# Moving convolutions between the stages of a pipelined Haar-mixing network: four channels come a batch earlier, empty ticks take put-off convolutions, and the last mixing has its first products ahead of its second ones

## The chip, the cores and the metric

The kernel runs on one core of a Trainium2 chip. Its engines work side by side[...]: PE (TensorE, the matmuls), DVE (VectorE), ACT (ScalarE), POOL (GpSimd, not used here) and SP (SyncE, which only issues transfers here; ACT issues some too). The metric is the device time of one execution in microseconds (us). The kernel before takes 2989.25 us, the median of three runs (2988.33 to 2990.84).

## The reference

The input x has 4 batches of 64 channels of 256 x 256 fp32 values. Four layers follow one another. Layers 0, 1 and 3 are long convolutions of each channel with a kernel that is an outer product of two filters, so that each is two triangular Toeplitz products, along one axis and then along the other:

```python
hx = _implicit_filter(z, Xw1, ..., t, deltas)      # 256 positions x 64 channels, from a small sine network
hy = _implicit_filter(z, Yw1, ..., t, deltas)
k = jnp.einsum('ijk,imk->ijmk', hx, hy)[0]         # one 256 x 256 kernel per channel
k_f = jnp.fft.rfft2(k, s=(512, 512)) / 512
u_f = jnp.fft.rfft2(x, s=(512, 512))
y = jnp.fft.irfft2(u_f * k_f, s=(512, 512))[..., :256, :256]
out = y + x * bias[:, None, None]
```

Layer 2 works on the 2-D Haar transform and mixes the 64 channels of a batch, so it needs all channels of the batch:

```python
f1 = haar2d(x)
for i in range(2):
    f4 = jnp.einsum('bchw,oc->bohw', f1 * v[i], conv_w[i])
    acc = acc + jnp.sign(f4) * jax.nn.relu(jnp.abs(f4) - tau[i])
y = haar2d(acc, inverse=True) + x
```

## The kernel before, in words

**Stages.** Each batch goes through three stages. `convolutions` does layers 0 and 1 for each channel and the forward Haar transform, and writes the Haar coefficients to DRAM (`coef`) and what the skip connection needs to `keep`. `mixing` does the channel mixing of layer 2 in 64 groups of four rows of coefficients, and adds the results up in the large tile `z`, which lies in SBUF. `inverse` takes one channel after the other out of `z`, does the inverse Haar transform, adds the skip connection and does layer 3 (`last`), or puts layer 3 off: it then stores the channel to `late`, and `convolution` does layer 3 later, under the mixing of another batch. `put_off` says which channels: every third from channel 2 on, 21 in each of batches 0 to 2, 63 in all.

**One convolution layer** is two contractions (`contract`, L186): `first` multiplies by one Toeplitz matrix on PE into a bank `pa` of PSUM, and ACT copies it to `a` (L198); `second` multiplies `a` by the other matrix into `py`, and DVE adds the bias term (L211). A contraction is four matmuls in source, two of 256 and two of 128 columns (L189, L190); [...] a contraction is eight instructions in the profile. The Toeplitz tile (`t`) is loaded by SP from the padded filter in DRAM. A channel of `convolutions` has four contractions, a put-off convolution two. The channel of `convolutions` also has a step of Haar sums on DVE (`pairs`, L256 and L257; the other levels by groups of four channels, `levels`, L266 and L267), a split of the result into two parts (`split`, L277 on ACT, L278 on DVE), and the transform along the partitions on PE (`down`, L285, copied by ACT at L293, stored by SP at L294).

**One group of mixing** is `mix` (four matmuls, L334, into `px`, which has two buffers; then a scaling of `px` into `f4`, of which DVE does the first part, L351, and ACT `n_act` of 16 slices, L353), `shrink` (Abs and Sign on ACT, L359 and L360; subtraction on DVE, L361), `signed` (DVE, L366) and `add` (DVE, into `z`, L370). `n_act` is 12 for batches 0 to 2 and 6 for batch 3. `mag` and `f4` have two buffers.

**One channel of inverse** is `fetch` (load of `r` from `keep`, and ACT takes the channel out of `z` as `zc`, L387), `rows` (PE, `pw`, L394 and L395; ACT and DVE split it, L397 and L398), `cols` (PE, `pu`, L407; DVE adds the skip, L411, and interleaves, L414 and L415), then `last` or the store to `late`. Before channel 0, `butterfly` (L219 to L221) combines the two halves of `z`.

**The order** is written out by hand in ticks: `at(tick, place, run, unit)` collects every step, and at the end of the kernel the steps are sorted by tick, then by place, and run in that order; the recording layer below still moves instructions of an engine past one another where their inputs allow. `mixing(b, start, ...)` puts group g at tick `start + g`. `spread(begin, end, n)` spreads n units evenly over ticks. The convolutions of batch b + 1 are spread over the ticks of the mixing of batch b, so that PE, DVE and ACT have both kinds of work; the 63 put-off convolutions are spread over the last mixing, since there are no further batches. With the numbers of this kernel:

| batch | mixing, ticks from start to end | under it | ticks of these |
|---|---|---|---|
| 0 | 77 to 144 | 64 convolutions of batch 1 | 64 to 145, 82 ticks |
| 1 | 208 to 275 | 64 convolutions of batch 2 | 205 to 276, 72 ticks |
| 2 | 339 to 406 | 64 convolutions of batch 3 | 336 to 407, 72 ticks |
| 3 | 470 to 537 | 63 put-off convolutions | 468 to 538, 71 ticks |

So eight ticks of 72 have no new convolution in the mixing of batches 1 and 2. The inverse of batch b begins at the end of its mixing. `after` (inside `convolutions`) spreads the Haar steps of the last two groups of channels threefold where they come after `border`, the end of the mixing: they then lie between channels of the inverse. Buffers that the change concerns: `in` (three: loads of x and of `late`), `toep` (five), `co` (two: coefficients on the way to `coef`, and `y3` on the way to the output), `sp` (one), `y` (three).

Of the kernel before, what the change touches and what calls it, by code (L numbers as in the profile page):

```python
# [9 lines left out]
F32 = mybir.dt.float32  # L10
# [6 lines left out]
B, C, S, EMB, ORD = 4, 64, 256, 33, 64  # L17
P = 128
ROW = S + P

GT = 4
BUFS = {"res": 1, "y": 3, "co": 2}

INV_2PI = float(np.float32(1.0 / (2.0 * math.pi)))
# [13 lines left out]
def conv_seq_kernel(ctx, tc, x, fz, fw, bias, decay, haar, haar_row, factors, vt, taut, wmix, out):  # L38
# [14 lines left out]
    nc = tc.nc  # L53

    const = ctx.enter_context(tc.tile_pool(name="const", bufs=1))
# [8 lines left out]
    psx = ctx.enter_context(tc.tile_pool(name="psx", bufs=2, space=PSUM))  # L64


    hbt = const.tile([P, P], F32, name="hbt")
    hb = const.tile([P, P], F32R, name="hb")
    hbr = const.tile([P, P], F32R, name="hbr")
    hrow = const.tile([P, 2, P], F32, name="hrow")  # L70
# [7 lines left out]
    sd = zpool.tile([P, 8, 2, 2, P], F32, name="sd")  # L78
    keep = [dram.tile([C, P, 2, 2, P], F32, name=f"keep{b}") for b in range(B)]
    coef = [dram.tile([2, C, P, S], F32, name=f"coef{b}") for b in range(B)]  # L80
    scales = dram.tile([S // 4 // GT, P, 2, GT, 16], F32, name="scales")
    pads = [dram.tile([C, 2, ROW], F32, name=f"pad{layer}") for layer in range(3)]
# [7 lines left out]
    def part(n, parts=P):  # L90
        free[0] += n
        return room[:parts, free[0] - n : free[0]]
# [52 lines left out]
        return [load, *steps, end, warm]  # L145

    def constants():
        signs = part(P)
        nc.sync.dma_start(hbt, haar[0])
        nc.sync.dma_start(signs, haar[1])  # L150
        nc.sync.dma_start(hrow, haar_row)
        nc.vector.memset(wb, 0.0)
        for r in range(2):
            nc.sync.dma_start(wb[r * C : (r + 1) * C, r, :], wmix)
        nc.scalar.copy(hb, signs)
        nc.scalar.copy(hbr, hbt)

    def tables():
# [10 lines left out]
        def scale(i):  # L169
            nc.vector.tensor_mul(vts[:, i], vts[:, i], fac[:, i])  # L170
            nc.sync.dma_start(
                scales[:, :, i].rearrange("n p g j -> p n (g j)"), vts[:, i].rearrange("p (n g) j -> p n (g j)", g=GT)
            )
# [12 lines left out]
    def contract(ps, src, t):  # L186

        for m in range(2):
            nc.tensor.matmul(ps[:, m, :], src[:, 0, m * P : (m + 1) * P], t[:, ::-1], start=True, stop=False)  # L189
            nc.tensor.matmul(ps[:, m, P:], src[:, 1, m * P : (m + 1) * P], t[:, : P - 1 : -1], start=False, stop=True)  # L190
# [12 lines left out]
    def second(b, st, key, layer, res, new, tag, ahead=None):  # L203
        def run(c):
# [4 lines left out]
            contract(ps, s[key], s[layer][:, 1, :])  # L209
            y = io.tile([P, 2, S], F32, name=f"{new}_{b}_{c}", tag=tag, bufs=BUFS[tag])  # L210
            nc.vector.scalar_tensor_tensor(y, s[res], bsb[:, layer, c : c + 1], ps, ALU.mult, ALU.add)  # L211
# [15 lines left out]
    def at(tick, place, run, unit):  # L227
        events.append((tick, place, len(events), run, unit))
# [5 lines left out]
                if stage is not None:  # L234
                    at(tick + s, -s, stage, unit)

    def convolutions(b, ticks, in_parts=(), border=None):


        st = {}  # L240

        def after(tick, n):
            return tick if border is None or tick < border or n < C // 4 - 2 else border + 3 * (tick - border)

        def load(c):
            xt = io.tile([P, 2, S], F32, name=f"x_{b}_{c}", tag="in", bufs=3)
            nc.sync.dma_start(xt, x[b, c].rearrange("(k p) w -> p k w", p=P))
            st[c] = {"x": xt, 0: toeplitz(0, c, f"t0_{b}_{c}")}

        last_second = second(b, st, "a1", 1, "y0", "y1", "res")  # L250

        def pairs(c):
            last_second(c)
            v = st.pop(c)["y1"].rearrange("p k (w e) -> p k w e", e=2)
            t = sd[:, c % 8]
            nc.vector.tensor_add(t[:, :, 0, :], v[:, :, :, 0], v[:, :, :, 1])  # L256
            nc.vector.tensor_sub(t[:, :, 1, :], v[:, :, :, 0], v[:, :, :, 1])  # L257
            nc.scalar.dma_start(keep[b][c], t)

        def levels(steps):  # L260
            def run(n):
                t = sd[:, n % 2 * 4 : n % 2 * 4 + 4]
                for step in steps:
                    v = t[:, :, :, 0, :].rearrange("p c k (w e) -> p (c k) w e", e=2 * step)
                    even, odd = v[:, :, :, 0], v[:, :, :, step]
                    nc.vector.tensor_sub(odd, even, odd)  # L266
                    nc.vector.scalar_tensor_tensor(even, even, 2.0, odd, ALU.mult, ALU.subtract)  # L267

            return run

        parts = {}

        def split(c):

            w = parts[c] = mx.tile([P, 2, 2, S], F32R, name=f"sp_{b}_{c}", tag="sp", bufs=1)
            t = sd[:, c % 8].rearrange("p k e w -> p k (e w)")
            nc.scalar.copy(w[:, 0], t)  # L277
            nc.vector.tensor_tensor(w[:, 1], t, w[:, 0].bitcast(F32), ALU.subtract)  # L278

        def down(c):  # L280
            ps = bank(f"pz_{b}_{c}")
            flat = "p k w -> p (k w)"
            if c in in_parts:
                for i in range(2):
                    nc.tensor.matmul(  # L285
                        ps.rearrange(flat), hbr, parts[c][:, i].rearrange(flat), start=(i == 0), stop=(i == 1)
                    )
            else:
                nc.tensor.matmul(
                    ps.rearrange(flat), hbt, sd[:, c % 8].rearrange("p k e w -> p (k e w)"), start=True, stop=True  # L290
                )
            t = io.tile([P, 2, S], F32, name=f"co_{b}_{c}", tag="co", bufs=BUFS["co"])
            nc.scalar.copy(t, ps)  # L293
            nc.sync.dma_start(coef[b][:, c].rearrange("k p w -> p k w"), t)  # L294

        stream(
            [load, first(b, st, "x", 0, "a0"), second(b, st, "a0", 0, "x", "y0", "y", ahead=1), first(b, st, "y0", 1, "a1"), pairs],
            ticks,
        )
        for n in range(C // 4):  # L300
            end = ticks[4 * n + 3] + 4
            for s, steps in enumerate([(1,), (2, 4), (8, 16, 32, 64)]):
                at(after(end + 1 + s, n), 1, levels(steps), n)
            for j in range(4):
                if 4 * n + j in in_parts:
                    at(after(end + 3 + j, n), 2, split, 4 * n + j)
                at(after(end + 4 + j, n), 2, down, 4 * n + j)
        return after(ticks[-1] + 11, C // 4 - 1)

    def mixing(b, start, n_act):  # L310
# [3 lines left out]
        def load(g):  # L314
            f = mx.tile([P, 2, S], F32, name=f"f_{b}_{g}", tag="f", bufs=3)
            nc.sync.dma_start(f, coef[b].rearrange("k c p w -> (k c) p w")[:, 2 * g : 2 * g + 2])
            st[g] = {"f": f}
            if g % GT == 0:
                t = mx.tile([P, 2, GT, 16], F32, name=f"vt_{b}_{g}", tag="vt")
                nc.sync.dma_start(t, scales[g // GT])  # L320
                st["vt", g // GT] = t

# [54 lines left out]
    def inverse(b, start, put_off):  # L377
# [25 lines left out]
        def cols(c):  # L403
            ps = psm.tile([P, 2, 2, P], F32, name=f"pu_{b}_{c}", tag="mm")
            flat = "p m e w -> p (m e w)"
            for i in range(2):
                nc.tensor.matmul(  # L407
                    ps.rearrange(flat), hb, st[c]["w"][:, i].rearrange(flat), start=(i == 0), stop=(i == 1)
                )
            t = io.tile([P, 2, 2, P], F32, name=f"t_{b}_{c}", tag="res", bufs=BUFS["res"])  # L410
            nc.vector.scalar_tensor_tensor(t, st[c]["r"], 0.5, ps, ALU.mult, ALU.add)  # L411
            u = io.tile([P, 2, S], F32, name=f"u_{b}_{c}", tag="y", bufs=BUFS["y"])
            v = u.rearrange("p m (w e) -> p m w e", e=2)
# [16 lines left out]
    def last(b, st):  # L430
        return [
            first(b, st, "u", 2, "a3"),
            second(b, st, "a3", 2, "u", "y3", "co"),
            lambda c: nc.scalar.dma_start(out[b, c].rearrange("(k p) w -> p k w", p=P), st.pop(c)["y3"]),
        ]

    def convolution(which, ticks):

        for (b, c), tick in zip(which, ticks):
            st = {}  # L440

            def load(c, b=b, st=st):
                u = io.tile([P, 2, S], F32, name=f"v_{b}_{c}", tag="in", bufs=3)
                nc.sync.dma_start(u, late[b, c])
                st[c] = {"u": u, 2: toeplitz(2, c, f"t2_{b}_{c}")}

            for s, stage in enumerate([load, *last(b, st)]):
                at(tick + s, -s, stage, c)


    def spread(begin, end, n=C):
        return [begin + i * (end - begin - 1) // (n - 1) for i in range(n)]


    put_off = range(2, C, 3)

    one, two, three = filters(0, nc.scalar), filters(1, nc.scalar), filters(2, nc.sync)
    one[0]()
# [10 lines left out]
            at(tick, 3, lambda unit, do=do: do(), 0)  # L469

    groups = S // 4
    ready = convolutions(0, range(C), in_parts=range(C))
    ahead = C
    start = ready + 3
    for b in range(B):
        mixing(b, start, 12 if b + 1 < B else 6)
        end = start + groups + 3
        if b + 1 < B:
            ready = convolutions(b + 1, spread(ahead, end + 2), in_parts=range(C), border=end)
        else:  # L480
            convolution(
                [(i, c) for i in range(B - 1) for c in sorted(put_off)], spread(start - 2, end + 2, (B - 1) * len(put_off))
            )
        inverse(b, end, put_off if b + 1 < B else ())

        start = max(end + C, ready + 3)
        ahead = start - 3
    for _, _, _, stage, unit in sorted(events, key=lambda e: e[:3]):
        stage(unit)

# [108 lines left out]
```

## Time and profile before

| what | us |
|---|---|
| median of three runs | 2989.25 |
| profiled execution | 2989.2 |
| its span, first to last instruction | 2987.4 |
| PE busy | 2919.9 (98%) |
| DVE busy | 2551.9 (85%) |
| ACT busy | 2156.5 (72%) |
| first mix of batches 0, 1, 2, 3 starts at | 458.7, 1096.5, 1776.5, 2450.7 |
| last add of batches 0, 1, 2, 3 starts at | 877.9, 1554.5, 2234.3, 2733.7 |

The granted clock of TensorE was 1.00 over the span. Times inside the profile count from the first instruction. A row of the timeline has the start, the length, the engine, the line, the operation, output<-input with shapes, the number of instructions merged into the row, and in brackets the idle time ahead of it with what ended it. A row of the stage view has the stretch, the busy time of PE, PEld (weight loads), DVE, ACT and POOL with the number of instructions, TensorE's clock, the share of the DMA engines and GB/s. [...]

### The profile page before, as it was taken

The numbers are of one execution on the slowest core, as the hardware profiler recorded it, in microseconds if no ns is written. First come the engines' busy times: TensorE is split into PE (matmuls) and PEld (weight loads), VectorE is DVE, ScalarE is ACT, GpSimd is POOL, SyncE is SP. The second block draws the span as 40 slices with busy tenths as digits, with TensorE's granted clock in tenths as the row PEclk, the third lists the DMA queues.
The fourth block names the chain that finished last, engine by engine and source line by source line (L and its number), as shares of the span: only waits on it lengthen the run. The fifth ranks groups of instructions, "written<-read, shape, count | busy, mean of one in ns | idle before, by whom it ended". The sixth has DMA issues, their size and how long they took to land. (4 is left out here: it accounts for less than half of the span.)

```text
span 2987.4 us, 51999 instructions
## 1 busy us (share of the span) xinstructions
PE 2919.9 (98%) x16950; PEld 2610.5 (87%) x16950; DVE 2551.9 (85%) x4576; ACT 2156.5 (72%) x5005; POOL 0.2 (0%) x4
## 2 busy tenths in 40 slices
PE   7999999999999999999999999999999999999999
PEld 6899988888888888888888988888888988888998
DVE  4766778999998879999989879999998889998776
ACT  1333338999986758989886758989886768887554
POOL 0000000000000000000000000000000000000000
PEclk9999999999999999999999999999999999999999
DMA  4877777766667876676777776676677877777676
GB/s 146 245 234 229 230 231 210 210 200 199 210 201 243 249 219 203 207 209 203 208 213 236 253 224 196 209 211 204 206 211 235 255 238 231 231 232 220 212 210 187
DMA packets 562496, 649.72 MB, mean 217 GB/s; under 512 B 44369, under 2 KB 447412, under 8 KB 562100
## 3 DMA queue, kind: packets, MB, share of 16 engines
q1 hardware_dynamic: 446132, 494.94, 58.0%
q10 hardware_dynamic: 116096, 151.46, 14.2%
q8 instruction: 137, 2.24, 0.3%
q14 instruction: 131, 1.07, 0.1%
HBM read 426.77 MB, written 219.48 MB: 216 GB/s over the span
## 5 line engine op out<-in xcount | busy, mean ns | idle before, releaser
L189 PE MATMUL py<-t,a 128*128 128x256 f32 x3072 | 923.3, 382 | 17.8 <-ACT a L198 8.6
L198 ACT COPY a<-pa 128x512 f32<-128x512 f32 x768 | 473.3, 617 | 442.2 <-PE pa L190 298.2
L190 PEld LDWEIGHTS py<-t,a 128*128 128x128 f32 x3072 | 583.4, 190 | 79.3
L353 ACT ACTIVATE f<-px,vt 128x64 f32<-128x64 f32 x2688 | 589.7, 351 | 75.7 <-DVE f L351 75.3
L190 PE MATMUL py<-t,a 128*128 128x128 f32 x3072 | 590.0, 274 | 0.0
L189 PEld LDWEIGHTS py<-t,a 128*128 128x128 f32 x3072 | 491.6, 191 | 69.5 <-ACT a L198 32.0
L334 PE MATMUL px<-wb,f 128*128 128x256 f32 x2048 | 504.3, 382 | 19.6 <-ACT f L353 19.6
L334 PEld LDWEIGHTS px<-wb,f 128*128 128x128 f32 x2048 | 362.1, 190 | 67.2 <-ACT f L353 32.1
L361 DVE TENSOR_TENSOR mag<-mag,vt 128x1024 f32<-128x1024 f32 x256 | 312.7, 1222 | 18.8 <-ACT mag L359 16.6
L366 DVE SCALAR_TENSOR_TENSOR mag<-mag,f 128x1024 f32<-128x1024 f32 x256 | 312.8, 1222 | 4.4 <-DVE sd L266 0.3
L397 ACT CAST w<-pw 128x512 fp32r<-128x512 f32 x256 | 150.2, 587 | 226.5 <-PE pw L395 214.6
L189 PE MATMUL pa<-t,y 128*128 128x256 f32 x1024 | 306.6, 381 | 2.5 <-DVE y L211 1.6
L189 PE MATMUL pa<-t,x 128*128 128x256 f32 x1024 | 305.6, 380 | 1.5 <-issue 1.5
L359 ACT ACTIVATE mag<-f 128x1024 f32<-128x1024 f32 x256 | 282.9, 1105 | 21.1 <-DVE z L370 7.0
L387 ACT COPY zc<-z 128x512 f32<-128x512 f32 x256 | 282.4, 1104 | 2.3 <-ACT w L397 1.9
L360 ACT ACTIVATE f<-f 128x1024 f32<-128x1024 f32 x256 | 273.2, 1067 | 13.1 <-DVE sd L257 5.7
L278 DVE TENSOR_TENSOR sp<-sd,sp 128x512 fp32r<-128x512 f32 x256 | 176.6, 690 | 92.6 <-ACT sp L277 91.9
L211 DVE SCALAR_TENSOR_TENSOR y<-x,bsb,py 128x512 f32<-128x512 f32 x256 | 191.0, 746 | 55.5 <-PE py L190 48.7
L189 PE MATMUL pa<-t,u 128*128 128x256 f32 x772 | 232.8, 383 | 3.6 <-PE pu L407 3.5
L411 DVE SCALAR_TENSOR_TENSOR t<-r,pu 128x512 f32<-128x512 f32 x256 | 175.0, 684 | 59.4 <-PE pu L407 55.2
L190 PEld LDWEIGHTS pa<-t,x 128*128 128x128 f32 x1024 | 194.6, 190 | 26.3
L190 PEld LDWEIGHTS pa<-t,y 128*128 128x128 f32 x1024 | 194.5, 190 | 26.3
(65 smaller groups left out, 4471.6 us busy)
## 6 DMA issues: line engine op xcount, KB each, us to landing
t<-pad SPq DMA_DIRECT2D x768, 256.0 KB, 4.0
x<-in_x SPq DMA_DIRECT2D x256, 256.0 KB, 3.9
keep<-sd ACTq DMA_DIRECT2D x256, 256.0 KB, 2.9
coef<-co SPq DMA_DIRECT2D x256, 256.0 KB, 3.1
f<-coef SPq DMA_DIRECT2D x256, 256.0 KB, 4.0
r<-keep SPq DMA_DIRECT2D x256, 256.0 KB, 3.2
out_y<-y ACTq DMA_DIRECT2D x256, 256.0 KB, 3.7
late<-u ACTq DMA_DIRECT2D x63, 256.0 KB, 2.8
```

The lines of the kernel that those rows point to most:

```text
L189: nc.tensor.matmul(ps[:, m, :], src[:, 0, m * P : (m + 1) * P], t[:, ::-1], start=True, stop=False)
L190: nc.tensor.matmul(ps[:, m, P:], src[:, 1, m * P : (m + 1) * P], t[:, : P - 1 : -1], start=False, stop=True)
L198: nc.scalar.copy(a, ps)
L211: nc.vector.scalar_tensor_tensor(y, s[res], bsb[:, layer, c : c + 1], ps, ALU.mult, ALU.add)
L278: nc.vector.tensor_tensor(w[:, 1], t, w[:, 0].bitcast(F32), ALU.subtract)
L334: nc.tensor.matmul(ps[:, h, q, :], f[:, q, h * P : (h + 1) * P], wb.rearrange("p r n -> p (r n)"), start=True, stop=True,)
L353: nc.scalar.mul(f4[:, j], px[:, j], scale(g, 0)[:, j : j + 1])
L359: nc.scalar.activation(mag, f4, AF.Abs)
L360: nc.scalar.activation(f4, f4, AF.Sign)
L361: nc.vector.tensor_sub(mag, mag, over(g, 1, 16))
L366: nc.vector.scalar_tensor_tensor(mag, mag, 0.0, st[g]["f4"], ALU.max, ALU.mult)
L387: nc.scalar.copy(a, z[:, :, :, c].rearrange("p h (i k) -> p h k i", k=2))
```

## The change

- `EARLY = 4`: 68 convolutions are spread over the ticks of the mixing of batch 1, all 64 of batch 2 (ticks 205 to 271) and the first four of batch 3 (272, 273, 274, 276). The other 60 of batch 3 are spread over the same 72 ticks of batch 2's mixing as before.
- The 12 ticks of these 72 without a convolution (341, 347, ..., 401, 406) each start a put-off convolution.
- Batch 0 puts off the channels c with c % 5 in (2, 4), 25 instead of 21; batches 1 and 2 put off 21 as before. Of the 67 put-off convolutions 12 go into these ticks and 55 under the last mixing.
- `convolution` takes the places of its four steps. Under batch 2's mixing they are (0, -1, -2, -3) for load, first, second and store, as before; under the last mixing (0, -2, -1, -3), so that a tick's first product stands ahead of `mix`, and its second product after it.
- `after` works with several borders: for each, the last two groups of four channels whose ticks lie before it are spread behind it. The call for batch 2 gives no border any more; that for batch 3 gives the ends of the mixings of batches 1 and 2.
- `hbt` becomes a piece of the scratch room inside `z`; the branch of `down` without parts, which no call used, is gone.

```diff
-    def convolutions(b, ticks, in_parts=(), border=None):
+    def convolutions(b, ticks, borders=()):
...
         def after(tick, n):
-            return tick if border is None or tick < border or n < C // 4 - 2 else border + 3 * (tick - border)
+            for border in borders:
+                left = sum(t < border + 2 for t in ticks) // 4
+                if left - 2 <= n < left and tick >= border:
+                    return border + 3 * (tick - border)
+            return tick
...
-    def convolution(which, ticks):
+    def convolution(which, ticks, places):
...
-            for s, stage in enumerate([load, *last(b, st)]):
-                at(tick + s, -s, stage, c)
+            for s, (place, stage) in enumerate(zip(places, [load, *last(b, st)])):
+                at(tick + s, place, stage, c)
...
-    put_off = range(2, C, 3)
+    put_off = [[c for c in range(C) if c % 5 in (2, 4)], range(2, C, 3), range(2, C, 3), ()]
+    deferred = [(b, c) for b in range(B) for c in put_off[b]]
...
+        if b == 0:
+            ahead = spread(begin, ends[0] + 2)
+            ready.append(convolutions(1, ahead, borders=ends))
+        elif b == 1:
+            ahead = spread(begin, ends[1] + 2, C + EARLY)
+            ready.append(convolutions(2, ahead[:C]))
+            ahead = ahead[C:]
+        elif b == 2:
+            more = spread(begin, ends[2] + 2, C - EARLY)
+            ready.append(convolutions(3, ahead + more, borders=ends[1:]))
+            gaps = sorted(set(range(begin, ends[2] + 2)) - set(more))
+            convolution(deferred[: len(gaps)], gaps, (0, -1, -2, -3))
+            deferred = deferred[len(gaps) :]
+        else:
+            convolution(deferred, spread(start - 2, ends[3] + 2, len(deferred)), (0, -2, -1, -3))
+        inverse(b, ends[b], put_off[b])
```

More of the change, by code (lines that the diff above doesn't have):

```diff
@@ L21 @@
 GT = 4
+EARLY = 4
 BUFS = {"res": 1, "y": 3, "co": 2}
@@ L64, in conv_seq_kernel @@
     psx = ctx.enter_context(tc.tile_pool(name="psx", bufs=2, space=PSUM))
-    hbt = const.tile([P, P], F32, name="hbt")
     hb = const.tile([P, P], F32R, name="hb")
@@ L147, in constants @@
     def constants():
-        signs = part(P)
+        signs, hbt = part(P), part(P)
         nc.sync.dma_start(hbt, haar[0])
@@ L282, in down @@
             flat = "p k w -> p (k w)"
[L283 to L291, printed above, removed]
+            for i in range(2):
+                nc.tensor.matmul(ps.rearrange(flat), hbr, parts[c][:, i].rearrange(flat), start=(i == 0), stop=(i == 1))
             t = io.tile([P, 2, S], F32, name=f"co_{b}_{c}", tag="co", bufs=BUFS["co"])
@@ L304, in convolutions @@
             for j in range(4):
-                if 4 * n + j in in_parts:
-                    at(after(end + 3 + j, n), 2, split, 4 * n + j)
+                at(after(end + 3 + j, n), 2, split, 4 * n + j)
                 at(after(end + 4 + j, n), 2, down, 4 * n + j)
@@ L471, in conv_seq_kernel @@
     groups = S // 4
-    ready = convolutions(0, range(C), in_parts=range(C))
-    ahead = C
-    start = ready + 3
+    ready = [convolutions(0, range(C))]
+    begin = C
+    start = ready[0] + 3
+    ends, ahead = [], []
     for b in range(B):
+        ends.append(start + groups + 3)
         mixing(b, start, 12 if b + 1 < B else 6)
-        end = start + groups + 3
-        if b + 1 < B:
[L479 to L487, printed above, removed]
+        if b == 0:
[14 more added lines that the diff above has]
+        inverse(b, ends[b], put_off[b])
+        if b + 1 < B:
+            start = max(ends[b] + C, ready[b + 1] + 3)
+            begin = start - 3
     for _, _, _, stage, unit in sorted(events, key=lambda e: e[:3]):
```

## The prediction

> **What bounds the kernel now.** I read the busy shares first, then the busy times stage by stage, then the timeline inside two stages, and at last the order of instructions of both programs on each engine.
>
> ```profile
> PE 2919.9 (98%) x16950; PEld 2610.5 (87%) x16950; DVE 2551.9 (85%) x4576; ACT 2156.5 (72%) x5005; POOL 0.2 (0%) x4
> ```
>
> PE (TensorE) is the bound on the whole. Both programs hold the same 2811 us of PE work (matmuls times the spacing below), so the change can only alter the time that PE loses. The stages, with start:end, PE, PEld, DVE and ACT busy:
>
> ```profile
> 945.00:1095.00 150.00, 150.00 (x954) 135.15 (x953) 123.74 (x234) 100.30 (x141) 0.00 (x0) 1.00 0.80 243
> 1100.00:1540.00 440.00, 432.96 (x2409) 384.64 (x2408) 408.73 (x714) 387.81 (x1092) 0.00 (x0) 1.00 0.69 205
> 1780.00:2220.00 440.00, 432.90 (x2411) 384.91 (x2410) 409.09 (x715) 388.04 (x1093) 0.00 (x0) 1.00 0.70 205
> 2450.00:2734.00 284.00, 276.75 (x1486) 243.56 (x1485) 276.89 (x325) 242.32 (x573) 0.00 (x0) 1.00 0.79 232
> 2745.00:2980.00 235.00, 235.00 (x1505) 216.80 (x1504) 169.59 (x315) 134.10 (x185) 0.00 (x0) 1.00 0.68 206
> ```
>
> The first and last rows are inverse stages (batches 0 and 3): PE never stops. The second and third are the mixing of batches 1 and 2, the fourth is the last mixing, where DVE (VectorE) is as full as PE. Busy time hides part of PE's loss, since a matmul of 256 columns is shown as 0.38 us while the next starts 0.217 us later (128 columns: 0.110). So I counted loss from start to start, as what exceeds that spacing: 25 us up to 130 us, 18.0 in the mixing of batch 0, 13.3 in batch 1's, 13.1 in batch 2's, 15.3 from 2450 to 2740, some 21 around these.
>
> Where a convolution's tick is empty, two mixes stand close on PE:
>
> ```profile
> 1403.97 1.89 PE L334 MATMUL px<-wb,f 128*128 128x256 f32 x8
> 1406.63 1.13 PE L334 MATMUL px<-wb,f 128*128 128x256 f32 x4 [0.77 <-ACT f L353]
> 1407.60 0.59 PE L189 MATMUL py<-t,a 128*128 128x256 f32 x2
> ```
>
> The second waits until ACT has emptied one of the two px buffers. Ticks that hold a whole convolution lose nothing: their px starts lie 7.43 us apart, the sum of their matmuls. In the last mixing DVE sets the pace:
>
> ```profile
> 2604.47 0.69 DVE L370 TENSOR_TENSOR z<-mag 128x512 f32<-128x512 f32 x1
> 2605.07 1.22 DVE L366 SCALAR_TENSOR_TENSOR mag<-mag,f 128x1024 f32<-128x1024 f32 x1
> 2606.21 0.75 DVE L211 SCALAR_TENSOR_TENSOR y<-v,bsb,py 128x512 f32<-128x512 f32 x1
> 2606.86 1.23 DVE L361 TENSOR_TENSOR mag<-mag,vt 128x1024 f32<-128x1024 f32 x1
> 2608.00 0.83 DVE L351 TENSOR_TENSOR f<-px,vt 128x640 f32<-128x640 f32 x1
> 2608.73 0.69 DVE L370 TENSOR_TENSOR z<-mag 128x512 f32<-128x512 f32 x1
> ```
>
> From add to add there is no gap: 4.26 us, of which the put-off convolution's y takes 0.66 (start to start) and the mixing 3.605. Nine ticks with eight convolutions need 9 x 3.605 + 8 x 0.657 = 37.7 us of DVE, 9 x 1.73 + 8 x 2.62 = 36.5 of PE, and take 38.1. The end of the stage:
>
> ```profile
> 2733.69 0.69 DVE L370 TENSOR_TENSOR z<-mag 128x512 f32<-128x512 f32 x1
> 2736.58 2.05 ACT L387 COPY zc<-z 128x512 f32<-128x512 f32 x2
> 2739.46 0.39 PE L394 MATMUL pw<-hrow,zc 128*128 128x128 f32 x2
> ```
>
> [...] after waits of 3 to 5 us:
>
> ```profile
> 23.89 5.00 PE L142 MATMUL warm<-z 128*128 128x256 f32 x12
> 29.91 2.43 PE L142 MATMUL warm<-z 128*128 128x256 f32 x10 [0.58 <-DVE z L133]
> ```
>
> That is 0.42 us a matmul, then 0.24.
>
> **The change, part by part.** A contraction (first or second product) is 4 x 0.217 + 4 x 0.110 = 1.31 us of PE.
>
> 1. Batch 0 puts off 25 channels instead of 21: its inverse loses 4 x 2.62 = 10.5 us of PE, and gets four stores to late instead of stores to out_y, as large and on the same queue. PE is 100% busy there (DVE 82%), so the stage shortens by 10.5.
> 2. The mixing of batch 1 takes 68 convolutions in 72 ticks instead of 64: 4 x (4 x 1.31 + 0.5) = +22.9 us of PE. SP issues 20 more transfers of 256 KB, with DMA at 69%. The stage takes the PE work in full.
> 3. The mixing of batch 2 takes 60 instead of 64 convolutions, and 12 put-off ones in the empty ticks: 12 x 2.62 - 22.9 = +8.5. Each put-off one brings two loads on SP, a copy of about 0.5 us and an output issue of 0.4 on ACT, a y of 0.66 on DVE. ACT gets 12 x 0.9 = 10.8 and loses four convolutions at about 2.6; DVE gets 7.9 and loses 4 x 4: both come out level or lighter.
> 4. The last mixing has 55 instead of 63: -8 x 2.62 = -20.9.
>
> The sum of 1 to 3 is +20.9 ahead of the last mixing, and 4 takes it back. In the built order the PE work ahead of the first mix of batch 3 is 2329.9 instead of 2309.0, which confirms it. What counts is how much of the -20.9 the last mixing returns, and what the filled ticks save.
>
> 5. Last mixing: DVE still has 64 x 3.605 us, and within the stage 54 y's instead of 60 (counted in the order): 6 x 0.657 = -3.9. From the last add to the first pw it was 5.77 us, because y's, a copy and two contractions stood in between. In the new order pw follows the last px directly and no y stands there: rest of the add and butterfly 1.3, zc 1.1, a hand-over, about 2.8. So -3.0.
> 6. The same fact costs something: the convolutions are finished early, the last six mixes follow one another, and PE has nothing from the last px to pw, some 13 us (three ticks of DVE at 3.6 and the 2.8). If its clock drops, the inverse starts at half speed. At the start of the trace the slow spell lasted from 22.0 to some 28.5 us, a loss of 3.2. Bounds 0 and 3.2; I take 1.7.
> 7. First products ahead of second ones: PE and ACT have room in this stage, and DVE's list of work is unchanged, so 0. DVE's gaps in the stage are 6.4 us, so it can't gain more than that; DVE waiting for a py behind a waiting px could lose about as much. Bounds -6 and +6.
> 8. Filled ticks. Batch 1 has three back-to-back mixes in the new order instead of seven. Apart from 0.9 at the stage's start its 13.3 are 1.8 for each, so -7.0 (bounds -13 and -3). Batch 2 has nine instead of seven: a half-filled tick still leaves two mixes together. Batch 0, which has 16 such places, lost 1.1 at each. So 9 x 1.1 to 9 x 1.8 = 9.9 to 16.2 against 13.1: I take 0, bounds -9 and +5. Nothing else is there to wait on but the shared co buffers: an out_y in flight (3.7 us to land) can hold ACT's coefficient copy, and behind it the copies of a that py waits for. ACT idles a tenth of this stage, and this is part of the +5.
> 9. The last two groups' Haar levels of batch 2 aren't spread over the inverse any more, and the first group of batch 3 comes there: DVE is at 90% around 1620. +1, bounds -2 and +4.
> 10. hbt in the scratch room and the dead branch of down: nothing at run time; one load more or less waits on no path.
>
> Sum: +20.9 - 3.9 - 3.0 + 1.7 + 0 - 7.0 + 0 + 1.0 = **+9.7 us**. The profiled execution took 2989.2 (span 2987.4 and 1.8 around it), the median of the runs is 2989.25. So **2999**.
>
> **Rivals.**
> (a) *The filled ticks pay for it.* Fixed is 20.9 - 3.9 - 3.0 + 1.7 = +15.7; with batch 1's loss gone but 1 (-12) and batch 2's down by two fifths (-5), plus 1: -0.3, so about 2989, no change. For it: 26.4 us of loss to be had. Against it: nine back-to-back mixes in batch 2.
> (b) *Faster: the last mixing is bound by PE and its hand-overs, not by DVE.* Place: 2450 to 2740. Many ticks last 4.35 us, which is exactly 1.73 + 2.62 of PE. If PE sets it and the new order keeps it so, the stage returns all 20.9 and, with -7.0 and +1, the time is 2974 to 2984, so about 2982. It decides from the point where a tick with three convolutions in four takes less than 3.605 + 0.75 x 0.657 = 4.10 us, and DVE's fullness (276.89 busy of 284) excludes nearly all of it.
> (c) *More waits.* The co buffers, the unspread levels and a DVE held by PE's order reach their upper bounds: 5 + 3 + 4 more, about 3010.
>
> **Numbers.** My forecast 0.64, (a) 0.18, (b) 0.07, (c) 0.11. It holds 2993 to 3005 on its own. The range is 2987 to 3009: it takes in (a) and part of (c). A measurement tells 0.2% (6 us) from no change: faster below 2983.3, slower above 2995.2. Faster 0.07 (b). Same 0.23: (a) and a small part of mine. Slower 0.70.
>
> **What would show it.** Right: the first px of batch 3 starts some 15 us later (about 2466); batch 1's mixing has half the waits of L334 on L353, batch 2's about as many as now; the last mixing has DVE without gaps, px starts about 4.1 us apart, PE idle shown there up by over 10 us, with one hole over 10 us ahead of pw. Wrong: PE's loss in batch 2's mixing nearly gone (then a), the last mixing shorter by more than 10 us (b), ACT waiting for out_y in batch 2's mixing or DVE gaps in the last (c).

## The result, and the profile after

The changed kernel takes 3009.24 us (median of four runs, 3007.01 to 3010.50), against 2990.05 us for the kernel before, measured beside it. The ratio is 1.0065, with an interval from 1.0053 to 1.0077: 19.2 us slower, where the forecast was 9.7 us slower and its range ended at 3009. The profiled execution has a span of 3008.7 us, 21.3 more than before.

The shares of busy time, from the page of the changed kernel, hide the difference:

```profile
PE 2924.3 (97%) x16950; PEld 2616.7 (87%) x16950; DVE 2554.5 (85%) x4576; ACT 2163.2 (72%) x5004; POOL 0.2 (0%) x4
```

The number of matmuls is the same, and so is the bound. What changed is seen stage by stage. The view is that of the busy times per stretch (start:end, length, PE, PEld, DVE, ACT and POOL busy with the number of instructions, TensorE's clock, DMA share, GB/s), here for the mixing of batch 1, of batch 2, the last mixing, the hand-over to the last inverse, its first 10 us, and its rest:

```profile
1090.00:1550.00 460.00, 455.44 (x2553) 407.76 (x2552) 425.00 (x748) 400.26 (x1108) 0.00 (x0) 1.00 0.70 208
1788.00:2233.00 445.00, 443.49 (x2481) 396.13 (x2480) 406.17 (x697) 389.08 (x1092) 0.00 (x0) 1.00 0.71 213
2466.00:2746.00 280.00, 260.02 (x1377) 229.81 (x1375) 263.48 (x306) 231.78 (x550) 0.00 (x0) 0.99 0.76 218
2746.00:2758.00 12.00, 0.23 (x2) 0.00 (x0) 10.86 (x15) 8.19 (x19) 0.00 (x0) 0.68 0.07 22
2758.00:2768.00 10.00, 9.87 (x47) 9.08 (x48) 4.57 (x8) 6.36 (x9) 0.00 (x0) 0.70 0.25 79
2768.00:3000.00 232.00, 232.00 (x1487) 214.09 (x1487) 167.91 (x312) 132.33 (x184) 0.00 (x0) 1.00 0.69 206
```

Three things are to be seen. In batch 2's mixing PE is now full. In the last mixing DVE is busy for 263.48 us of 280, where it had 276.89 of 284: the engine that sets the pace there now has gaps. And after a hole on PE its clock is 0.70 for the first 10 us of the inverse.

Put together from the starts of the first mix of each batch, the first `pw` and the last add:

| part of the span | before | after | difference | forecast |
|---|---|---|---|---|
| up to the first mix of batch 3 | 2450.7 | 2465.5 | +14.8 | +14.9 |
| last mixing, first mix to last add | 283.0 | 290.7 | **+7.7** | **-3.9** |
| last add to first `pw` of batch 3 | 5.8 | 2.0 | -3.8 | -3.0 |
| first `pw` to the end | 247.9 | 250.5 | +2.6 | +1.7 |
| span | 2987.4 | 3008.7 | +21.3 | +9.7 |

The whole error is in one row, the last mixing: 11.6 us. The waits of DVE in that stage (line waited for: us in total, times, longest) name what it lacked. First the kernel before, from 2450 to 2734 us, then the one after, from 2465 to 2757:

```profile
DVE y L211 <- PE py L190: 2.1, 4, 0.7
```

```profile
DVE y L212 <- PE py L191: 10.7, 10, 3.1
```

DVE waits for the second product of put-off convolutions. The waits of PE in the same stage say why that product is late:

```profile
PE px L331 <- ACT f L350: 8.7, 5, 2.6
PE pa L190 <- DMA v<-late: 8.2, 8, 2.8
PE pa L190 <- issue: 2.3, 1, 2.3
```

The second row has no counterpart in the kernel before: the first product (`pa`) waits for its input `v` to arrive from `late`. (`issue` in the third stands for a wait whose cause the profile doesn't show.) One of these waits in the timeline of the kernel after (rows between them left out):

```profile
2645.41 0.74 DVE L212 SCALAR_TENSOR_TENSOR y<-v,bsb,py 128x512 f32<-128x512 f32 x1
...
2646.18 0.33 SPq L441 DMA_DIRECT2D v<-late  x1
...
2651.09 0.85 PE L190 MATMUL pa<-t,v 128*128 128x256 f32 x2 [2.79 <-DMA v<-late]
...
2653.01 2.81 PE L331 MATMUL px<-wb,f 128*128 128x256 f32 x8
...
2657.39 0.75 DVE L212 SCALAR_TENSOR_TENSOR y<-v,bsb,py 128x512 f32<-128x512 f32 x1 [3.14 <-PE py L191]
```

A `y` on DVE is the last reader of its `v` and so frees one of the three `in` buffers. Only then does SP issue the next load from `late` (2646.18). The first product that needs it can start only 4.9 us later, and PE has stood idle for 2.79 us by then. The mix and the second product stand behind that `pa` in PE's list, and are late too: ACT has copied the second product's input by 2648.93 (a copy of 0.59 us from 2648.34), but PE starts it at 2655.88, and DVE waits 3.14 us for it. The mix after the wait is also slow: its eight matmuls take from 2653.01 to 2655.66, 0.33 us each on average in place of 0.217, and the granted clock is 0.50 from 2651.45 to 2654.85. One ring is closed: `y` frees the buffer, the load fills it, `pa` and `py` make a later `y`, which frees a buffer for another load. The new places shorten the load's lead at both ends: they put `pa` ahead of `mix`, and `py`, which the freeing `y` waits for, behind it.

### The profile page after: what moved, and what is told of

Read it like the earlier page. It is cut to its first block, busy times and chain, and to the rows that moved or that the text cites. A ratio compares the mean times of both kernels' runs of the same rounds, so it can differ in the third digit from the quotient of the medians.

```text
span 3008.7 us, 52020 instructions
## 1 busy us (share of the span) xinstructions
PE 2924.3 (97%) x16950; PEld 2616.7 (87%) x16950; DVE 2554.5 (85%) x4576; ACT 2163.2 (72%) x5004; POOL 0.2 (0%) x4
## 5 line engine op out<-in xcount | busy, mean ns | idle before, releaser
L331 PE MATMUL px<-wb,f 128*128 128x256 f32 x2048 | 498.2, 382 | 15.9 <-ACT f L350 15.7
L357 ACT ACTIVATE f<-f 128x1024 f32<-128x1024 f32 x256 | 273.7, 1069 | 33.5 <-DVE y L212 13.2
```

What stands on the lines that cost most here:

```text
L331: nc.tensor.matmul(ps[:, h, q, :], f[:, q, h * P : (h + 1) * P], wb.rearrange("p r n -> p (r n)"), start=True, stop=True,)
L357: nc.scalar.activation(f4, f4, AF.Sign)
```

## The experiments

My theory after the result was this ring: the new places bring the first product nearer to its load, whose issue is tied to an earlier `y`. The rivals were that the order costs time on PE itself whatever the buffers are; that the 8 convolutions moved out of the last mixing cost more than was forecast; and that the hole and the clock behind it are the cause. Ratios are to the kernel before, run beside each group (2987.94, 2987.93 and 2989.12 us).

**The old places in the last mixing, all else changed.**

```diff
-            convolution(deferred, spread(start - 2, ends[3] + 2, len(deferred)), (0, -2, -1, -3))
+            convolution(deferred, spread(start - 2, ends[3] + 2, len(deferred)), (0, -1, -2, -3))
```

> The changed kernel with the old order in the last mixing (second products ahead of first ones), all else as changed. Theory A (the new order is what lengthened the last mixing: a put-off convolution's load of late can only start when the y three convolutions earlier has freed its buffer, and its first product now comes too early after that): PE's waits on v<-late (8.2 us in the changed kernel) vanish, from the first mix of batch 3 to the last add it takes about 279 us instead of 290.7, and PE has work again behind the last px, so that its clock stays up: some 2997. Theory B (the fewer put-off convolutions or the new spread lengthened it, not the order): the stage stays near 290 and the time near 3009.

Measured: 2995.58 us, ratio 1.0025 [1.0015, 1.0036]. The last mixing takes 279.3 us, against a forecast of 279.1, and the mean granted clock of the profiled execution is 1.0, where the changed kernel has 0.997. PE's waits there, from 2466 to 2746 us, have no load in them. Those on ACT hardly reach DVE, which waits only 0.8 us for a `py` in the stage and sets the pace:

```profile
PE px L331 <- ACT f L350: 14.1, 18, 1.6
PE py L190 <- ACT a L199: 4.7, 7, 1.5
```

So the order costs the 11.4 us between 290.7 and 279.3, and the step on DVE's work was right. The rest of the change still costs 7.6 us.

**The new order alone, in the kernel before.**

```diff
-    def convolution(which, ticks):
+    def convolution(which, ticks, places):
...
-            for s, stage in enumerate([load, *last(b, st)]):
-                at(tick + s, -s, stage, c)
+            for s, (place, stage) in enumerate(zip(places, [load, *last(b, st)])):
+                at(tick + s, place, stage, c)
...
-                [(i, c) for i in range(B - 1) for c in sorted(put_off)], spread(start - 2, end + 2, (B - 1) * len(put_off))
+                [(i, c) for i in range(B - 1) for c in sorted(put_off)], spread(start - 2, end + 2, (B - 1) * len(put_off)), (0, -2, -1, -3)
```

> The kernel before with the new order in the last mixing alone (first products ahead of second ones), 63 put-off convolutions as before. Theory A: the loads of late come too late here as well, the last mixing grows by 8 to 14 us, 2997 to 3004, and PE waits on v<-late. Theory B: the order is neutral, 2988 to 2992.

Measured: 3004.41 us, ratio 1.0053 [1.0038, 1.0068]; the last mixing takes 304.7 us, 21.7 more than before. With 63 convolutions in place of 55, 20 waits for a load are listed instead of 8. PE's waits from 2447 to 2752 us, the largest row:

```profile
PE pa L189 <- DMA v<-late: 16.1, 20, 1.7
```

The order does the harm without any other part of the change: 21.7 us here with 63 convolutions in the stage, 11.4 with 55.

**The new order with more room for the loads.** The tiles `v` of the last mixing take turns between the `in` buffers and the three of `y`, which otherwise stand free for part of that stage. No instruction moves.

```diff
-    def convolution(which, ticks, places):
+    def convolution(which, ticks, places, tags=("in",)):
...
+            tag = tags[i % len(tags)]
...
-                u = io.tile([P, 2, S], F32, name=f"v_{b}_{c}", tag="in", bufs=3)
+                u = io.tile([P, 2, S], F32, name=f"v_{b}_{c}", tag=tag, bufs=3)
...
-            convolution(deferred, spread(start - 2, ends[3] + 2, len(deferred)), (0, -2, -1, -3))
+            convolution(deferred, spread(start - 2, ends[3] + 2, len(deferred)), (0, -2, -1, -3), ("in", "y"))
```

> The changed kernel, in which the put-off convolutions of the last mixing take their input in turn from the buffers named in and from those named y, which are idle in this stage: twice as many buffers, the same order of products. Theory A: loads of late no longer wait for y, PE's waits on v<-late vanish, the last mixing takes 279 to 282 us; the hole ahead of the inverse and the clock drop behind it remain; about 2998. If the order harms in another way (PE's or DVE's list itself): no change from 3009. Theory B: no change either.

Measured: 2997.58 us, ratio 1.0031 [1.0022, 1.0040]; the last mixing takes 279.0 us. PE's waits from 2466 to 2746 us:

```profile
PE px L331 <- ACT f L350: 9.7, 8, 2.6
PE pa L190 <- PE pa L191: 0.6, 1, 0.6
```

The waits for `v<-late` are gone, with the new order still there, and so are DVE's waits for `py`. This settles it: in this stage the order by itself is free, the lead of the load is what it used up. SP still waits for a `y` before such loads, 59.0 us in all, but the load has time to land. Taken load by load from the traces of the last mixing, a load of `late` is issued 9.6 us (median) before its first product starts with the old places, 5.1 us with the new ones, and 18.1 us with the new ones and both sets of buffers; to land it takes some 4 us in all three (medians of 3.6, 4.1 and 3.8).

**The same pair without the rest of the change**: the new order with both sets of buffers, in the kernel before (`convolution` edited as in the two runs above).

```diff
-                [(i, c) for i in range(B - 1) for c in sorted(put_off)], spread(start - 2, end + 2, (B - 1) * len(put_off))
+                [(i, c) for i in range(B - 1) for c in sorted(put_off)], spread(start - 2, end + 2, (B - 1) * len(put_off)), (0, -2, -1, -3), ("in", "y")
```

> The kernel before with the new order and two sorts of buffers for the put-off inputs. Theory A: without the wait for buffers the new order is harmless: the last mixing from first px to last add takes 281 to 285 us instead of 304.7, the time is 2986 to 2990. If the new order then also removes DVE's remaining gaps (6 us), as low as 2983. If another harm of the order was hidden under the loads: above 2993.

Measured: 2988.58 us, ratio 1.0000 [0.9991, 1.0009]. The last mixing is 284.8 us (+1.8), the hand-over 3.8 shorter, the inverse 1.6 longer. The order gains nothing either: what it saves at the hand-over it pays in the inverse (from 2350 us on, the longest `pw` matmul takes 0.58 us, in the kernel before 0.28), and in the stage. PE's waits from 2446 to 2733 us have one row:

```profile
PE pa L189 <- PE pa L190: 1.0, 1, 1.0
```

**The hole ahead of the inverse, filled** in the kernel with both sets of buffers. Six added matmuls, whose results nothing uses, and the convolutions behind them give PE work there.

```diff
+        def fill(g):
+            f4, ps = st[g]["f4"], bank(f"fill_{b}")
+            for i in range(6):
+                nc.tensor.matmul(
+                    ps[:, i % 2, :],
+                    f4[:, :2].rearrange("p j o -> p (j o)"),
+                    f4[:, :4].rearrange("p j o -> p (j o)"),
+                    start=True,
+                    stop=True,
+                )
...
+        if b == B - 1:
+            at(start + 63, 6, fill, 62)
```

> As the run with two sorts of buffers, with six more matmuls (2.6 us of PE, their result is not used) that read the scaled group 62 of the last mixing, so that PE has work between the last px and the first pw. Theory C (the tail from the first pw to the end is longer by 1.6 to 2.6 us because PE's clock dropped in the hole): the tail is back at 247.9 to 248.3 us instead of 249.5, and the granted clock at its beginning stays at 1. If the tail is long for another reason, such as an inverse that starts with empty buffers, it stays at 249.5. The whole time hardly moves, 2995 to 2999, since the added work and the convolutions behind it delay the first pw by about as much.

Measured: 2997.51 us, ratio 1.0031 [1.0020, 1.0042]. The stretch around the hand-over, first without and then with the filler (columns as in the stage view above; the third number from the end is the clock):

```profile
2747.00:2757.00 10.00, 10.00 (x55) 9.15 (x56) 5.36 (x10) 6.82 (x9) 0.00 (x0) 0.82 0.37 96
```

```profile
2745.00:2757.00 12.00, 12.00 (x81) 11.13 (x81) 7.59 (x13) 7.95 (x12) 0.00 (x0) 1.00 0.56 175
```

The clock is at 1.00 there and the inverse takes 247.6 us in place of 249.5, so the longer inverse does come from the clock. But the first `pw` now starts 6.5 us after the last add instead of 2.0. No time is won.

**The 8 convolutions given back to the last mixing.** From the kernel with the old places: batches 1 and 2 put off 25 channels as batch 0 does, so that 12 fill the empty ticks and 63 remain for the end.

```diff
-    put_off = [[c for c in range(C) if c % 5 in (2, 4)], range(2, C, 3), range(2, C, 3), ()]
+    put_off = [[c for c in range(C) if c % 5 in (2, 4)]] + 2 * [[c for c in range(C) if c % 5 in (2, 4)]] + [()]
```

> The changed kernel with the old order, and batches 1 and 2 put off 25 channels as batch 0 does, so that 63 instead of 55 put-off convolutions stand under the last mixing; four full convolutions early and twelve in the empty ticks as changed. If the step of the forecast holds that a put-off convolution costs the last mixing 0.66 us of DVE and PE elsewhere 2.62: this is 8 x 2 = 16 us below the run with the old order and 55, less about 3 for the longer hand-over: about 2983, below the kernel before, which shows what the filled ticks are worth by themselves. If the last mixing gives back the full PE time of a convolution, it equals the run with 55.

Measured: 2985.60 us, ratio 0.9992 [0.9983, 1.0001]. It is as fast as the kernel before, and 10.0 us faster than with 55 in the last mixing. The last mixing takes 283.5 us again, and the first mix of batch 3 starts at 2451.9 in place of 2466.5. (Each of these is from one profiled execution, of 2990.89 and 2999.32 us, against medians of 2985.60 and 2995.58, so they are uncertain by some us.) That is the price of moving PE work out of a stage that DVE sets: 8 x 2.62 = 21.0 us of PE ahead of the last mixing bring 4.2 back in it. The start of batch 3 gains 14.6 and not 21.0, since the inverses of batches 1 and 2 now lose 9.8 and 7.5 us, where they lost 6.0 and 4.2. PE's waits from 1576 to 1782 us:

```profile
PE pa L190 <- ACT co L291: 2.5, 1, 2.5
PE pa L190 <- PE pu L404: 1.7, 3, 0.8
```

**The Haar levels of batch 2 spread again**, both last groups, in the kernel of the last experiment.

```diff
-            ready.append(convolutions(2, ahead[:C]))
+            ready.append(convolutions(2, ahead[:C], borders=ends[1:]))
```

> As the run with 63 under the last mixing, with the Haar levels of batch 2's last two groups of channels spread over the inverse again, as in the kernel before. If the unspread levels cost the transition from batch 1's mixing to its inverse (the forecast took 1, up to 4): 2981 to 2984, and PE loses 5 to 7 us from the first pw of batch 1 to the first px of batch 2 instead of 9.8. If the extra loss there comes from the pattern of put-off channels or from the early group itself: no change from 2985.6, within 1.5.

Measured: 2983.03 us, ratio 0.9984 [0.9977, 0.9991]. PE's loss in the inverse of batch 1 falls from 9.8 to 6.9 us. The spread of the fifteenth group puts its Haar steps behind the first sums of batch 3 in the same slots, so that four channels of batch 2 are transformed from overwritten values; the number and kind of the instructions is the same.

**Only the last group spread**, again with 63 in the last mixing.

```diff
-    def convolutions(b, ticks, borders=()):
+    def convolutions(b, ticks, borders=(), spread_groups=2):
...
-                if left - 2 <= n < left and tick >= border:
+                if left - spread_groups <= n < left and tick >= border:
...
-            ready.append(convolutions(2, ahead[:C]))
+            ready.append(convolutions(2, ahead[:C], borders=ends[1:], spread_groups=1))
```

> As the run with 63 under the last mixing, with the Haar levels of batch 2's last group alone spread over the inverse. (With two groups spread, the fifteenth group's steps came behind the first sums of batch 3 in the same slots of sd, so that run transformed four channels of batch 2 from overwritten values; its instructions and times were the same in kind.) If the unspread levels cost what that run saved: from the first pw of batch 1 to the first px of batch 2 PE loses 7 to 8.5 us instead of 9.8, and the time is 2983 to 2985, below the kernel before by some 4. If the gain needs both groups: 2985.6, no change.

Measured: 2982.09 us (13 runs), ratio 0.9976 [0.9967, 0.9984]. This version is faster than both kernels, by 7.0 and about 27 us. The page's busy line, and PE's waits in the inverse of batch 1 (1574 to 1776 us):

```profile
PE 2918.6 (98%) x16950; PEld 2611.3 (88%) x16950; DVE 2549.8 (86%) x4576; ACT 2164.6 (73%) x5004; POOL 0.2 (0%) x4
```

```profile
PE pa L190 <- issue: 1.1, 1, 1.1
PE py L190 <- DVE y L212: 0.7, 1, 0.7
```

PE's wait of 2.5 us on the coefficient copy (`co`) is gone (one of 0.2 us is left), and the loss there is 5.8 us, less than the 7 to 8.5 expected.

**Without the four early channels**, from the kernel with 63 in the last mixing and no group spread: `EARLY = 0`, eight empty ticks filled, and 71 channels put off (25, 23 and 23).

```diff
-EARLY = 4
+EARLY = 0
...
-    put_off = [[c for c in range(C) if c % 5 in (2, 4)]] + 2 * [[c for c in range(C) if c % 5 in (2, 4)]] + [()]
+    put_off = [[c for c in range(C) if c % 5 in (2, 4)]] + 2 * [sorted([*range(2, C, 3), 16, 40])] + [()]
```

> As the run with 63 under the last mixing, but no channel of batch 3 comes early: 64 convolutions under each mixing as in the kernel before, the eight empty ticks under batch 2's mixing take put-off ones (25, 23 and 23 put off in batches 0, 1, 2; 63 stay for the last mixing). It tells apart which part earned the 11 us that PE loses less in the two mixings. If the early channels and the filled ticks each earn their part: batch 1's mixing loses 13.3 us again (9.2 with early ones), batch 2's some 6, and the time lies between 2985 and 2990. If filling alone does it all and the early channels only cost in the inverse of batch 1: 2981 to 2985.

Measured: 2997.20 us, ratio 1.0032 [1.0020, 1.0043], worse than was expected. Batch 1's mixing has its waits back (13.1 us of loss). The surprise is the inverse of batch 1, with 13.6 us of loss; PE's longest wait there (1556 to 1785 us) is for the split of Haar sums:

```profile
PE pz L289 <- ACT sp L282: 2.9, 1, 2.9
```

All 64 channels of batch 2 then run to tick 276, and their last groups' steps meet the inverse without being spread; that this is the cause is argued, not shown. The place of these groups and the pattern of put-off channels changed with the early channels, so the run doesn't price the latter.

**Another pattern of put-off channels** in the fastest version: every third and four more, as many as there.

```diff
-    put_off = [[c for c in range(C) if c % 5 in (2, 4)]] + 2 * [[c for c in range(C) if c % 5 in (2, 4)]] + [()]
+    put_off = [[c for c in range(C) if c % 5 in (2, 4)]] + 2 * [sorted([*range(2, C, 3), 10, 25, 40, 55])] + [()]
```

> The same with another choice of the 25 channels that batches 1 and 2 put off: every third, as in the kernel before, and four more between. If the pattern with two of five (put-off ticks close together) is what costs PE 3 us more in the inverses of batches 1 and 2 than in the kernel before, they fall to some 5 and 4 us and the time by 3 to 5; if the number of put-off channels is what counts, no change within 1.5 us.

Measured: 2990.62 us, ratio 1.0007 [0.9999, 1.0015]: 8.5 us slower than the even pattern, the opposite of what was expected. PE's loss in the inverses of batches 1 and 2 is 10.3 and 12.1 us instead of 5.8 and 6.9. PE's waits in that of batch 1 (1574 to 1780 us):

```profile
PE pa L190 <- PE pu L404: 4.9, 6, 0.9
PE pu L404 <- DVE w L395: 1.2, 2, 0.6
```

Where two neighbouring channels are put off (10 and 11, for one), less PE work lies between their short chains. That this is why PE waits is argued, not shown.

## Why the prediction was wrong

**The step that failed is item 7**, first products ahead of second ones, costed at 0 with 6 as its upper bound. It measured 11.6 us in the profile (11.4 against the old places; 12 by the two ratios, 1.0065 and 1.0025, of 2990). The forecast said that PE and ACT have room and that DVE's list of work is unchanged. Both hold. It didn't follow the moved contraction's inputs: the two loads on SP ahead of it, and the `in` buffer that the load needs. With the first product ahead of the mix and the second behind it, a load that a `y` releases, and that takes 4.1 us to land in the median (3.1 to 5.7), is often too late. The mechanism named for the upper bound was half right: DVE did wait for a `py`, for 10.7 us, but that `py` stood behind a `pa` without data, not behind a waiting `px`. The forecast looked at the buffers of `px` and `co`; those that ran short were of `in`: with a second set PE's 8.2 us of waits for loads are gone.

**Items 1 to 4 and 8 to 9, up to the first mix of batch 3**: +14.8 us for a forecast of +14.9, but the terms differ. Relative to the +20.9 of moved work, batch 1's mixing lost 3.9 us less, not 7.0 (item 8). Its waits of `px` on ACT are gone altogether, but waits of `py` on copies of ACT, 1.4 us before, doubled. The waits of PE in the kernel before, 1100 to 1540 us, and in the one after, 1100 to 1550:

```profile
PE px L334 <- ACT f L353: 5.0, 7, 0.8
PE py L189 <- ACT a L198: 1.4, 6, 0.6
```

```profile
PE py L190 <- ACT a L199: 2.7, 8, 0.7
```

Batch 2's mixing lost 7.3 us less, where I had taken 0. The close pairs of mixes are there, in both batches and as many as forecast (three and nine), but they hardly wait. From the timeline of the kernel after, one pair in batch 1 and one in batch 2, and the waits of PE in batch 2 from 1790 to 2233 us:

```profile
1211.36 3.12 PE L331 MATMUL px<-wb,f 128*128 128x256 f32 x12
...
1949.46 2.32 PE L331 MATMUL px<-wb,f 128*128 128x256 f32 x10
```

```profile
PE px L331 <- ACT f L350: 0.6, 2, 0.4
PE py L190 <- ACT a L199: 0.6, 1, 0.6
```

Counted from start to start, the first pair loses 0.26 us and the second none, where the pair in the forecast shows an idle time of 0.77. All nine places of batch 2 together lose 1.3 us in this way, the worst 0.6. So item 8 took the neighbourhood of two mixes for the cost, with a price of 1.1 to 1.8 us a place; it is no sufficient cause. What makes one pair wait and another not was not tested.

What I gave as a sign of rival (a), PE's loss in batch 2's mixing nearly gone, so came true by more than half (13.1 to 5.8), without bringing its time. The inverses took back 1.5, 1.4 and 0.6 us, 3.5 in place of item 9's 1. These terms come to +13.2; the other 1.6 us I can't attribute. That the whole fits the forecast to 0.1 us is luck. How far one profile can be trusted here: the two kernels with only the new order (with and without the second set of buffers) don't differ from the kernel before up to that point, and start the first mix of batch 3 at 2446.9, 3.8 us earlier; most of that arises ahead of the first inverse. So the fit to 0.1 us lies far inside what a repeat would scatter.

**Item 5** held: 279.3 and 279.0 us for a forecast of 279.1 once the load is out of the way, and -3.8 for -3.0 at the hand-over. **Item 6** held in kind: +2.6 for +1.7, within its bounds (+1.6 behind the same hole with both sets of buffers). That the clock might drop in the hole was an estimate. Its bound of 3.2 was taken from the start of the trace, where no matmul ran at full speed before the slow ones (pairs of 256 columns take 1.22 and 1.06 us at 22.02 and 23.04, and one takes 0.59 at 28.73; the view gives a granted clock of 1.00 from 22.00 to 28.50): that shows a slow start, not the drop of a PE that was at speed. The timeline of the kernel after shows the hole and half speed behind it:

```profile
2756.17 0.69 DVE L367 TENSOR_TENSOR z<-mag 128x512 f32<-128x512 f32 x1
...
2757.03 2.02 ACT L384 COPY zc<-z 128x512 f32<-128x512 f32 x2 [2.74 <-DVE z L222]
...
2758.13 0.79 PE L391 MATMUL pw<-hrow,zc 128*128 128x128 f32 x2 [11.90 <-ACT zc L384]
...
2759.57 1.06 PE L190 MATMUL py<-t,a 128*128 128x256 f32 x2
...
2764.20 0.59 PE L190 MATMUL pa<-t,v 128*128 128x256 f32 x2
```

Two matmuls take 1.06 us at 2759.57 and 0.59 at 2764.20; the granted clock is 0.50 from 2758 to 2764.

**The rivals.** (b) falls: with the load out of the way the last mixing returned 3.7 to 4.0 of the 20.9 us, and giving the work back to it made the kernel 10.0 us faster. (a) had the direction (11.2 us less loss in the two mixings, where it counted on 17), but not the sum, because a part came back in the inverses and PE's moved work stayed. (c) named about the right time, 3010, and one of its parts, a DVE held by PE's order, is the nearest to what happened, and its sign, gaps on DVE in the last mixing, came true; but it was priced at 4 (although item 7's own bound was 6) and measured at 11.6. Its other parts came in part or not at all: no wait of ACT for an `out_y` is listed in batch 2's mixing, and the inverses gave 3.5 us, 2.5 above the sum's 1, for the 3 that (c) added.

## What to carry to other kernels

When an instruction is moved earlier, look at when its inputs are requested, and what frees the buffers they land in: if a consumer further down the same chain frees them, the move takes from the load's lead (here from 9.6 us to 5.1 in the median), and what stands behind the waiting instruction in its engine's list is late with it (here a mix and a second product, for which DVE waited 3.14 us). Work moved out of a stage buys only what the stage's own bound gives back: 21 us of PE work taken from a stage that DVE sets returned 4. And work that fills empty ticks should not be taken from a stage that gives little back for it; here more put-off convolutions to fill the ticks, the last stage left full and the last Haar group spread gave 2982.09 us.

## What the runs showed of the hardware that was not expected

In the last mixing of the kernel after, the granted clock is 0.50 twice for 3.4 us: from 2651.45, 0.4 us after PE resumed from the wait of 2.79 us (matmuls of 256 columns then start 0.427 us apart), and from 2716.30, 1.1 us after it resumed from one of 2.34 us. After waits of 2.56 and 2.64 us in the same stage (until 2584.71 and 2737.42) the clock stays at 1.00. A wait of 2.34 us was thus followed by a drop and one of 2.64 us was not: the length of the one wait doesn't tell whether it comes, and what does is not shown. After the hole of 11.90 us PE was slow for some 6 us (to about 2764, at a granted clock of 0.50), and the inverse took 2.6 us longer than before. And the filler, with which the clock was at 1.00 again when the inverse began, won nothing, as the inverse then started 6.5 us after the last add instead of 2.0.
